# Row logits of a graph attention layer: turned on VectorE in 32x32 blocks instead of on TensorE

## The chip, the cores and the metric

The kernel runs on one core of a Trainium2 chip. The metric is the device time of one execution in microseconds (us). The engines are named as in the profile: PE is TensorE (PEld its weight loads), DVE is VectorE, ACT is ScalarE, POOL is GpSimd, SP is SyncE, which issues all the transfers that matter here.

## The reference

Two layers run over 64 graphs of 256 nodes with 512 features each. The first is a graph attention layer with 8 heads of 64 units, the second a transformer-like attention with the adjacency added to its probabilities. Each ends in a residual and a layer norm. The first layer is what the change touches:

```python
feats = jnp.einsum('bnf,hfu->bhnu', X, W)
e_self = jnp.einsum('bhnu,hu->bhn', feats, a_self)
e_neigh = jnp.einsum('bhnu,hu->bhn', feats, a_neigh)
dense = e_self[..., :, None] + e_neigh[..., None, :]
dense = jax.nn.leaky_relu(dense, negative_slope=0.2)
dense = dense + NEG_BIG * (1.0 - A[:, None, :, :])
att = jax.nn.softmax(dense, axis=-1)
out = jnp.einsum('bhij,bhju->bhiu', att, feats) + b[None, :, None, :]
...
x = _layernorm(x + _L0_gnn_ref(x, adj, ...), axis=-1)
x = _layernorm(x + _L1_gnn_ref(x, nodemask, adj, adj, ...), axis=-1)
```

Since the logit is a sum of one term per row and one per column, the exponential of the leaky sum is a product of a row factor and a column factor, and the larger of two such products. The kernel needs, for each head, the row factor exp(-0.8 (e_self + largest e_neigh)), limited to between 1e-30 and 1, on all 128 partitions, along the free dimension.

## The kernel before

Nodes lie on partitions in T = 2 tiles of 128 (P), features in C = 4 chunks. `proj0(b)` projects graph b for layer 0. Its result V0 holds, for each node and head, 64 features and two more columns: e_self and e_neigh. So the logits come out with nodes on partitions (columns), and the row factor must be turned so that nodes lie along the free dimension, and then be copied to all partitions.

From graph 2 on (62 graphs) this is done by these steps of `proj0`:

- `rows` (L551): eight matmuls against the identity write the logits of both kinds, turned, into a PSUM tile pr. Rows 0, 6, 12, ... hold e_self of the eight heads, rows 64 on hold e_neigh. VectorE takes the maximum (L560) and multiplies it by -0.8 (L561).
- `broadcast(0)` (L567): ScalarE takes the exponential, straight from PSUM, into the tile grow. The maximum rides along in its last column.
- `broadcast(1)` (L571 to L576): VectorE clamps grow. One transfer takes the eight rows to a DRAM buffer gs, a second one spreads gs over 128 partitions into gb (1 MB).
- `columns` (L645 on): nd is e_neigh less the maximum, and ScalarE makes the column factors ccol from it.
- `weights` of `attend0` (L741): VectorE makes the attention weights pT from gb, ccol and the adjacency; L764 multiplies them with v.

`shared` (L519 to L535) prepares the matrix ct of the second layer from the turned adjacency: part 0 is a sum and the tile even, part 1 two multiplications and another sum. `far` supplies exponentials of the adjacency for it.

The order of the work is written out by hand. `do(stage, b, step)` emits one step and `in_order` ties every instruction to the one before it on its engine, so each engine runs its instructions in the order of the source. `attention0_beside_projections1(b)` and `attention1_beside_projections0(b)` alternate for b from 2 to 63; one pair is one period of the kernel. A period works on four graphs at once: layer 0 of one, the projections of the next, and the layer-1 softmax and output of two earlier ones. In `second_beside_first` stands the order around the first of the 62 uses. The steps around the change, by their lines: `values` of `attend1` (L1054, av) and its copy oT (L1062); `scores` (L925, pz) and its exponentials (L944, p); `half_blocks` (L304 to L310, the sums oC of oT); `product` of `attend1` (L87, po, with the copies o at L340); `both` (L956) and its row sums pd (L964); `turned` xT (L130). Layer norms take three small POOL instructions each (L394 to L398), with the mean at L377.

Matrix products of the projections run as seven half-size products (`seven`), of which four in a row add into one PSUM bank; ScalarE copies the partial sum out between two of them, and the next product waits for that copy.

All DMA issues are on SP, in the order of the source: for one period the hidden rows hs out and back in blocks (hb), gs, gb, the next adjacency adj and mask, the reciprocals rs and their spread rb, the output, y, x and xb.

PSUM tiles of the kind that pr has come from a ring of four (tag mm).

Of the kernel before, what the change touches and what calls it, by code (L numbers as in the profile page):

```python
# [8 lines left out]
FT = mybir.dt.float32  # L9
BF = mybir.dt.bfloat16  # L10
U8 = mybir.dt.uint8
AF = mybir.ActivationFunctionType
ALU = mybir.AluOpType
AX = mybir.AxisListType
# [3 lines left out]
def kernel(  # L18
# [29 lines left out]
    nc = tc.nc  # L48
    P = 128
    NB, N, F = x.shape  # L50
    H, _, U = w0.shape
    T = N // P
# [3 lines left out]
    UX = U + 2  # L56
    W = 6
    R = W * (H - 1) + 1
    NEG = 1e10
    HIDE = 2.0**100  # L60
    TINY = 1e-30
# [4 lines left out]
    consts = ctx.enter_context(tc.tile_pool(name="consts", bufs=1))  # L66
# [10 lines left out]
    def ps_tile(shape, name):  # L77

        return psum.tile(shape, FT, tag="mm", name=name, bufs=4)

    matmul = nc.tensor.matmul
# [35 lines left out]
    B = 32  # L117
    Q = P // B
# [83 lines left out]


    maskz = io.tile([NB, N], FT, tag="y", name="maskz", bufs=1)
    hide = consts.tile([P, T, NB], FT, name="hide")
    m33 = consts.tile([P, T, NB], FT, name="m33")
    MASK = {}
# [280 lines left out]
    def proj0(b):  # L488
# [25 lines left out]

        def shared(part=None):
            mrow = FAR[1]
            if part != 1:
                CT[b] = work.tile([P, T, N], FT, tag="ct", name=f"ct_{b}", bufs=3)
                nc.vector.tensor_add(CT[b], pa, FAR[0])  # L519
                FAR[2] = work.tile([P, N], FT, tag="far", name=f"even_{b}", bufs=1)  # L520
                nc.vector.tensor_scalar(
                    FAR[2], mrow, -LA / N, LA / N, op0=ALU.mult, op1=ALU.add
                )
            if part == 0:
                return
            for j in range(T):
                nc.vector.scalar_tensor_tensor(
                    CT[b][:, j, :],
                    CT[b][:, j, :],
                    m33[:, j, b : b + 1],  # L530
                    mrow,
                    op0=ALU.mult,
                    op1=ALU.mult,
                )
            nc.vector.tensor_add(  # L535
                CT[b], CT[b], FAR[2].unsqueeze(1).to_broadcast([P, T, N])
            )
# [6 lines left out]
                nc.scalar.copy(xT[:, :, t * P : (t + 1) * P], pt)  # L544

        def rows():
            pr = ps_tile([P, N], f"pr_{b}")
            for t in range(T):
                for s in range(2):
                    cols = V0[b][:, t].rearrange("p h u -> p (h u)")  # L550
                    matmul(  # L551
                        pr[s * U : s * U + R, t * P : (t + 1) * P],
                        cols[:, U + s : U + s + UX * (H - 1) + 1 : UX // W],
                        ident,
                        start=True,
                        stop=True,
                    )
            grow = small.tile([R, N + 1], FT, tag="grow", name=f"grow_{b}", bufs=1)
            nb = small.tile([R, 1], FT, tag="nb", name=f"nb_{b}", bufs=2)
            nc.vector.tensor_reduce(grow[:, N : N + 1], pr[U : U + R], AX.X, ALU.max)  # L560
            nc.vector.tensor_scalar_mul(nb, grow[:, N : N + 1], -0.8)  # L561
            ROW.update(logits=pr, rows=grow, shift=nb)

        def broadcast(part):
            grow = ROW["rows"]
            if part == 0:
                nc.scalar.activation(  # L567
                    grow[:, :N], ROW["logits"][:R], AF.Exp, bias=ROW["shift"], scale=-0.8
                )
                return  # L570
            nc.vector.tensor_scalar(  # L571
                grow[:, :N], grow[:, :N], 1.0, TINY, op0=ALU.min, op1=ALU.max
            )
            gs = dram.tile([H, N + 1], FT, tag="gs", name=f"gs_{b}")
            nc.sync.dma_start(gs, grow[0:R:W])
            nc.sync.dma_start(  # L576
                gb.rearrange("p h n -> p (h n)"),
                gs.rearrange("h n -> (h n)").partition_broadcast(P),
            )
# [11 lines left out]
                )  # L591

        def cleared():
            ROW["rows"] = small.tile([P, N + 1], FT, tag="grow", name=f"grow_{b}", bufs=1)
            nc.gpsimd.memset(ROW["rows"], 0.0)

        def maxima(part=None):

# [98 lines left out]
        def scaled(h):  # L697
# [15 lines left out]
            xT_rows=from_rows,  # L713
            aT=lambda: transpose_blocks(pa, ADJB[b]),
            rows=rows,
            broadcast=broadcast,
            columns=columns,
            far=far,
# [497 lines left out]
    def do(stage, b, step, *args):  # L1216

        if 0 <= b < NB:
            if (stage, b) not in S:
                S[stage, b] = stages[stage](b)  # L1220
            S[stage, b][step](*args)
            in_order()

    def start():
# [120 lines left out]
        for h in range(HG, H):  # L1345
            do("attend0", 1, "weights", h)
        do("proj0", 0, "shared", 1)
        do("proj0", 1, "far", 1)
        load_adj(2)
        do("proj1", 0, "qk", "p4")  # L1350
# [4 lines left out]
    def second_beside_first():  # L1355


        b = 1
        for g in range(2):
            for t in range(T):  # L1360
                do("attend0", b, "product", g, t)
        do("attend0", b, "rec0", 0)
        do("attend0", b, "rec0", 1)
        load_rowmask()
        nc.sync.dma_start(bo_bc, b_out.partition_broadcast(P))
        WO["12"] = load_wo()
        do("turned", 2, "xT")
        do("turned", 2, "xC")
        do("attend0", b, "norm0", 0, 0)
        do("proj1", 0, "values", "p1")  # L1370
        do("attend0", b, "norm0", 0, 1)
        for t in range(T):
            do("attend0", b, "norm0", 1, t)
        do("proj1", 0, "values", "p2")
        do("proj1", 0, "v_add", 11)
        do("attend0", b, "end")
        right_factors(wf_sb, wf12, (0, 1, 2))
        do("proj1", 0, "values", "p6")
        do("proj1", 0, "values", "p5")
        do("proj1", 0, "values", "p7")  # L1380
        do("proj1", 0, "v_add", 22)
        right_factors(wf_sb, wf12, (3,))
        load(3)
        do("proj0", 2, "product", "p1")
        do("proj1", 0, "values", "p4")
        do("attend0", b, "squares", slice(0, 1), False)
        do("proj0", 2, "product", "p6")
        do("attend0", b, "squares", slice(1, 2), slice(0, 2))
        do("proj1", 0, "values", "p3")
        do("proj0", b, "shared")  # L1390
        do("proj0", 2, "aT")
        do("proj1", 0, "v_add", 12)
        do("proj0", 2, "product", "p5")
        do("proj0", 2, "product", "p7")
        do("attend0", b, "norm")
        do("proj1", b, "blocks")
        do("proj0", 2, "add", 22)
        do("proj0", 2, "product", "p2")
        do("proj0", 2, "product", "p4")
        do("proj0", 2, "far")  # L1400
        do("proj0", 2, "product", "p3")
        do("proj0", 2, "add", 11)
        do("proj0", 2, "add", 12)
        do("proj1", b, "from_rows", 0)
        do("proj1", b, "from_rows", 1)
        do("proj0", 2, "shared", 0)
        do("proj0", 2, "rows")
        do("proj0", 2, "broadcast", 0)
        do("softmax1", 0, "scores", 0)
        do("proj0", 2, "broadcast", 1)  # L1410
        load_adj(3)
        do("softmax1", 0, "scores", 1)
        do("proj0", 2, "shared", 1)
        do("proj1", b, "hC")
        do("softmax1", 0, "both", 0)
        do("softmax1", 0, "scores", 2)
        do("softmax1", 0, "both", 1)
        do("softmax1", 0, "scores", 3)
        do("softmax1", 0, "both", 2)
        do("turned", 3, "xT")  # L1420
        do("softmax1", 0, "both", 3)
        do("proj1", b, "qk", "p1")
        do("proj1", b, "qk", "p2")
        do("proj0", 2, "bias")
        do("softmax1", 0, "sums")
        do("softmax1", 0, "invert")
        do("proj0", 2, "columns")
        do("softmax1", 0, "inverted")
# [85 lines left out]
    def attention1_beside_projections0(b):  # L1514


        do("attend1", b - 2, "values", 0)
        do("attend1", b - 2, "values", 1)
        do("proj0", b + 1, "shared", 0)
        do("proj0", b + 1, "rows")  # L1520
        do("attend1", b - 2, "values", 2)
        do("attend1", b - 2, "values", 3)
        do("proj0", b + 1, "broadcast", 0)
        do("softmax1", b - 1, "scores", 0)
        do("proj0", b + 1, "shared", 1)
        if b + 2 < NB:
            do("turned", b + 2, "xT")
        do("proj0", b + 1, "broadcast", 1)
        if b + 2 < NB:
            load_adj(b + 2)  # L1530
        do("softmax1", b - 1, "scores", 1)
        do("attend1", b - 2, "half_blocks", 0)
        do("softmax1", b - 1, "both", 0)
        do("attend1", b - 2, "half_blocks", 1)
        do("softmax1", b - 1, "scores", 2)
# [153 lines left out]
```

## Time and profile before

| | us |
|---|---|
| median of 3 runs | 2828.33 |
| lowest, highest | 2826.14, 2829.4 |
| the profiled execution, whole | 2827.07 |
| its span, first to last instruction | 2825.3 |
| period of the steady part | 43.12 |

| engine | busy us | share of the span |
|---|---|---|
| PE | 2802.8 | 99% |
| PEld | 2238.0 | 79% |
| DVE | 2564.2 | 91% |
| ACT | 1811.0 | 64% |
| POOL | 257.3 | 9% |

In a row of the groups, the columns are: line, engine and operation, output and inputs by name, shapes, count; then the busy time and the mean nanoseconds of one; then the idle time of the engine before them, with what ended it. In the timeline a line gives start, length, engine, line and names; the bracket at the end is the idle time before it and its releaser. Instructions of one engine overlap by some 0.08 us at their ends, so the distance from one start to the next is the cost to the engine, and it is a little less than the length.

### The profile page before, as it was taken

How to read it: one execution, taken by the hardware profiler on the slowest of the kernel's cores; microseconds unless marked ns; L12 is line 12 of the kernel's file. 1: busy time of each engine (PE TensorE's matmuls, PEld its weight loads, DVE VectorE, ACT ScalarE, POOL GpSimd, SP SyncE). 2: the span in 40 equal slices, each digit the busy share in tenths (PEclk: the TensorE clock that was granted, in tenths of full speed). 3: DMA queues.
4: the chain of work that ended last, by engine and by line, in shares of the span. 5: the costliest groups of instructions: out<-in, count | busy, mean ns of one | idle time of the engine just before them, and what ended most of it. 6: DMA issues, size and time to landing. Idle time of an engine off the chain costs nothing.

```text
span 2825.3 us, 93442 instructions
## 1 busy us (share of the span) xinstructions
PE 2802.8 (99%) x39080; PEld 2238.0 (79%) x39080; DVE 2564.2 (91%) x5140; ACT 1811.0 (64%) x5051; POOL 257.3 (9%) x534
## 2 busy tenths in 40 slices
PE   9999999999999999999999999999999999999998
PEld 7878878788787788788787877887878878778785
DVE  7999999999999999999999999999999999999984
ACT  4666666666666666666666666666666666666663
POOL 1000100010010001000100100010001001000101
PEclk9999999999999999999999999999999999999999
DMA  7444545445545445445455454454554544544531
GB/s 141 121 106 136 134 125 141 122 133 143 123 126 139 121 135 136 125 139 122 133 143 123 125 139 122 133 137 125 139 122 133 144 121 128 137 123 132 133 107 67
DMA packets 772433, 362.56 MB, mean 128 GB/s; under 512 B 688319, under 2 KB 690351, under 8 KB 756014
## 3 DMA queue, kind: packets, MB, share of 16 engines
q1 hardware_dynamic: 769902, 356.07, 48.1%
q8 instruction: 310, 5.08, 0.8%
q14 instruction: 109, 0.89, 0.1%
q10 hardware_dynamic: 2112, 0.52, 0.1%
HBM read 288.11 MB, written 68.13 MB: 126 GB/s over the span
## 4 chain that ended last, share of the span: by engine, by line
PE 96%; DVE 1%; DMA 1%; SPq 1%; ACT 1%; issue 0%; POOL 0%; DVEq 0%; POOLq 0%
PE pq_p L87 27%; PE po_p L87 14%; PE pf_p L87 14%; PE pv_p L87 13%; PE av L764 8%; PE pz L925 8%; PE av L1054 7%; PE pd L964 2%; PE pr L551 1%; PE po L87 0%; SPq L265 0%; DMA rb<-rs 0%; DMA wo_sb<-in_L_gnn_W_out_dram 0%; SPq L244 0%; SPq L123 0%
## 5 line engine op out<-in xcount | busy, mean ns | idle before, releaser
L87 PE MATMUL pq_p<-hC,wqk_sb 128*64 128x128 f32 x8192 | 470.7, 273 | 3.1 <-DVE wqk_sb L283 1.6
L87 PEld LDWEIGHTS pq_p<-hC,wqk_sb 128*64 128x64 f32 x8192 | 449.1, 137 | 5.0 <-issue 3.1
L741 DVE SCALAR_TENSOR_TENSOR pT<-gb,ccol,at 128x256 f32<-128x256 f32 x992 | 403.0, 477 | 17.2 <-ACT ccol L652 17.2
L87 PE MATMUL pq_p<-hT,wqk_sb 128*64 128x128 f32 x6144 | 358.2, 273 | 0.3 <-DVE qk L343 0.3
L87 PEld LDWEIGHTS pq_p<-hT,wqk_sb 128*64 128x64 f32 x6144 | 342.5, 137 | 10.3 <-issue 0.8
L944 ACT ACTIVATE p<-pz,hide 128x512 f32<-128x512 f32 x638 | 333.7, 629 | 8.0 <-PE pz L925 1.0
L1035 DVE TENSOR_TENSOR p<-p,rb 128x1024 f32<-128x1024 f32 x252 | 299.2, 1208 | 4.8 <-DMA rb<-rs 4.8
L1044 DVE TENSOR_TENSOR p<-p,ct 128x1024 f32<-128x1024 f32 x252 | 299.0, 1207 | 0.2
L785 ACT ACTIVATE x<-av,rec 128x64 f32<-128x64 f32 x1024 | 224.6, 336 | 64.3 <-DVE rec L777 64.3
L764 PE MATMUL av<-v,pT 128*64 128x65 f32 x8192 | 253.5, 222 | 1.3 <-issue 0.7
L87 PE MATMUL pf_p<-wf_sb,xC 128*64 128x264 f32 x1984 | 254.5, 386 | 0.0
L700 ACT ACTIVATE v<-v 128x64 f32<-128x64 f32 x1024 | 251.3, 337 | 2.6 <-DVE v L691 2.6
L764 PEld LDWEIGHTS av<-v,pT 128*64 128x64 f32 x8192 | 249.7, 138 | 3.4 <-issue 2.4
L87 PE MATMUL pv_p<-wv_sb,hC 128*64 128x256 f32 x2048 | 245.3, 380 | 3.7 <-ACT v L340 3.7
L340 ACT COPY qk<-pq_p 128x512 f32<-128x512 f32 x256 | 149.0, 582 | 152.7 <-PE pq_p L87 150.0
L1054 PE MATMUL av<-p,v 128*64 128x256 f32 x2016 | 240.6, 379 | 2.1 <-DVE p L1044 2.1
L925 PE MATMUL pz<-qk 64*128 64x256 f32 x2048 | 238.7, 383 | 0.0
L340 ACT COPY v<-pv_p 128x256 f32<-128x256 f32 x256 | 95.6, 373 | 222.0 <-PE pv_p L87 222.0
L394 POOL TENSOR_SCALAR rstd_l<-rstd_l 128x2 f32<-128x2 f32 (+1 forms) x130 | 96.8, 744 | 1534.1 <-ACT junk L383 1533.9
L87 PE MATMUL po_p<-wo_sb,oC 128*64 128x256 f32 x1984 | 235.2, 379 | 0.0
L925 PEld LDWEIGHTS pz<-qk 64*128 64x128 f32 x2048 | 192.3, 186 | 45.0 <-issue 24.6
L956 DVE SCALAR_TENSOR_TENSOR both<-p 128x512 f32<-128x512 f32 x256 | 172.4, 674 | 44.6 <-ACT p L944 44.2
(172 smaller groups left out, 4460.9 us busy)
## 6 DMA issues: line engine op xcount, KB each, us to landing
rb<-rs SPq DMA_DIRECT2D x63, 1024.0 KB
gb<-gs SPq DMA_DIRECT2D x62, 1028.0 KB
hs<-x SPq DMA_DIRECT2D x64, 512.0 KB
xb<-in_x_dram SPq DMA_DIRECT2D x252, 128.0 KB
x<-in_x_dram SPq DMA_DIRECT2D x63, 512.0 KB
y<-hs SPq DMA_DIRECT2D x63, 512.0 KB
out_dram<-y SPq DMA_DIRECT2D x63, 512.0 KB
hb<-hs SPq DMA_DIRECT2D x248, 128.0 KB
```

The source lines that it names most:

```text
L87: matmul(dst[cols], lhsT[:, cols], rhs, **flags)
L340: nc.scalar.copy(out[COPIES[p]], dst)
L700: nc.scalar.activation(v[:, :U], v[:, :U], AF.Copy, scale=v[:, U : U + 1])
L741: nc.vector.scalar_tensor_tensor(pT[h][:, j, :], GB[b][h], CCOL[b][:, j, h : h + 1], AT[b][:, j, :], op0=ALU.max, op1=ALU.mult,)
L764: matmul(av[r * half : (r + 1) * half, k, :], pT[h][:, j, i : i + half], V0[b][:, j, h, :UA], start=(j == 0), stop=(j == T - 1),)
L785: nc.scalar.activation(X1[b][:, t, h * U : (h + 1) * U], av[:, k, :U], AF.Copy, scale=REC0[g][:, t, k : k + 1],)
L925: matmul(pz[r][:, j, :], QK[b][rows, g, 1, j * P : (j + 1) * P], QK[b][rows, g, 0, :], start=True, stop=True,)
L944: nc.scalar.activation(to, of, AF.Exp, bias=hide[:, j, b : b + 1], scale=U**-0.5,)
L956: nc.vector.scalar_tensor_tensor(both[g], p[:, :, 0, :], TINY, p[:, :, 1, :], op0=ALU.add, op1=ALU.add)
L1035: nc.vector.tensor_mul(p, p, REC[b][:, k : k + 2, g // 2, :] .unsqueeze(2) .to_broadcast([P, 2, T, N]),)
L1044: nc.vector.tensor_add(p, p, CT[b].unsqueeze(1).to_broadcast([P, 2, T, N]))
L1054: matmul(av[0][r * U : (r + 1) * U, g % 2, :], V1[b][:, j, 2 * g + r, :], PROBS[b][g][:, r, j, :], start=(j == 0), stop=(j == T - 1),)
```

## The change

The eight matmuls and their PSUM tile are gone. VectorE copies the logits of all nodes from V0 into a tile of its own (col_t: two kinds, two node tiles, 32 columns of which 8 are heads), and turns it in 32x32 blocks into row_t. There, heads lie on the first 8 partitions of each of four quarters of 32 partitions, and each quarter holds a fourth of the nodes of each tile. VectorE reduces each quarter's e_neigh to a maximum; POOL copies the four quarters side by side on the first 32 partitions; VectorE reduces these to the maximum (`top`), in a new step `shift`; POOL multiplies it by -0.8 four times, once for each quarter, and a transfer takes the maximum to gs. ScalarE's exponential and the clamp then work on 128 partitions of 64 elements instead of 43 of 256. The rows go to gs in four transfers, one for each quarter.

The order moves too. `shared` has a third part, the last sum alone. `rows` comes ahead of `shared` part 0; then follow `scores` 0, `shared` 1, `shift`, `shared` 2, and only then the exponential, after those of `scores` 0. The clamp and the transfers to gs and gb, with the loads of adj and mask behind them, come after xT, the exponentials of `scores` 1 and the first three sums of `half_blocks`. In the first period hC is split in two, around the clamp. The tile grow becomes a constant, shared with the two graphs at the start.

```diff
+    grow_sb = consts.tile([P, N + 1], FT, name="grow_sb")
+    col_t = grow_sb[:, : N // 2].rearrange("p (s t h) -> p s t h", s=2, t=T)
+    row_t = grow_sb[:, N // 2 : N].rearrange("p (s t r) -> p s t r", s=2, t=T)
...
         def rows():
-            pr = ps_tile([P, N], f"pr_{b}")
-            for t in range(T):
-                for s in range(2):
-                    cols = V0[b][:, t].rearrange("p h u -> p (h u)")
-                    matmul(
-                        pr[s * U : s * U + R, t * P : (t + 1) * P],
-                        cols[:, U + s : U + s + UX * (H - 1) + 1 : UX // W],
-                        ident,
-                        start=True,
-                        stop=True,
-                    )
-            grow = small.tile([R, N + 1], FT, tag="grow", name=f"grow_{b}", bufs=1)
-            nb = small.tile([R, 1], FT, tag="nb", name=f"nb_{b}", bufs=2)
-            nc.vector.tensor_reduce(grow[:, N : N + 1], pr[U : U + R], AX.X, ALU.max)
-            nc.vector.tensor_scalar_mul(nb, grow[:, N : N + 1], -0.8)
+            if b == 2:
+                nc.gpsimd.memset(col_t, 0.0)
+            nc.vector.tensor_copy(
+                col_t[:, :, :, :H],
+                V0[b][:, :, :, U:].rearrange("p t h s -> p s t h"),
+            )
+            nc.vector.transpose(
+                row_t.rearrange("p s t r -> p (s t r)"),
+                col_t.rearrange("p s t h -> p (s t h)"),
+            )
+            quarter = small.tile([P, 1], FT, tag="quarter", name=f"quarter_{b}", bufs=2)
+            nc.vector.tensor_reduce(
+                quarter, row_t[:, 1].rearrange("p t r -> p (t r)"), AX.X, ALU.max
+            )
+            quarters = small.tile([B, Q], FT, tag="quarters", name=f"quarters_{b}", bufs=2)
+            for q in range(Q):
+                nc.gpsimd.tensor_copy(
+                    quarters[:, q : q + 1], quarter[q * B : (q + 1) * B]
+                )
+
+        def shift():
+            top = small.tile([B, 1], FT, tag="top", name=f"top_{b}", bufs=2)
+            nc.vector.tensor_reduce(top, ROW["quarters"], AX.X, ALU.max)
+            nb = small.tile([P, 1], FT, tag="nb", name=f"nb_{b}", bufs=2)
+            for q in range(Q):
+                nc.gpsimd.tensor_scalar_mul(nb[q * B : (q + 1) * B], top, -0.8)
+            gs = dram.tile([H, N + 1], FT, tag="gs", name=f"gs_{b}")
+            nc.sync.dma_start(gs[:, N : N + 1], top[:H])
 
         def broadcast(part):
             if part == 0:
-                nc.scalar.activation(
-                    grow[:, :N], ROW["logits"][:R], AF.Exp, bias=ROW["shift"], scale=-0.8
-                )
+                nc.scalar.activation(grow, grow, AF.Exp, bias=ROW["shift"], scale=-0.8)
                 return
-            nc.sync.dma_start(gs, grow[0:R:W])
+            nc.vector.tensor_scalar(grow, grow, 1.0, TINY, op0=ALU.min, op1=ALU.max)
+            for q in range(Q):
+                nc.sync.dma_start(
+                    gs[:, :N].rearrange("h (t q r) -> q h t r", q=Q, r=B)[q],
+                    grow[q * B : q * B + H],
+                )
...
     def attention1_beside_projections0(b):
+        do("proj0", b + 1, "rows")
         do("proj0", b + 1, "shared", 0)
-        do("proj0", b + 1, "rows")
         do("attend1", b - 2, "values", 2)
         do("attend1", b - 2, "values", 3)
-        do("proj0", b + 1, "broadcast", 0)
         do("softmax1", b - 1, "scores", 0)
         do("proj0", b + 1, "shared", 1)
+        do("proj0", b + 1, "shift")
+        do("proj0", b + 1, "shared", 2)
+        do("proj0", b + 1, "broadcast", 0)
         if b + 2 < NB:
             do("turned", b + 2, "xT")
+        do("softmax1", b - 1, "scores", 1)
+        do("attend1", b - 2, "half_blocks", 0)
         do("proj0", b + 1, "broadcast", 1)
         if b + 2 < NB:
             load_adj(b + 2)
-        do("softmax1", b - 1, "scores", 1)
-        do("attend1", b - 2, "half_blocks", 0)
```

More of the change, by code (lines that the diff above doesn't have):

```diff
@@ L516, in shared @@
             mrow = FAR[1]
-            if part != 1:
+            if part in (None, 0):
                 CT[b] = work.tile([P, T, N], FT, tag="ct", name=f"ct_{b}", bufs=3)
@@ L525, in shared @@
                 return
-            for j in range(T):
+            for j in range(T) if part != 2 else ():
                 nc.vector.scalar_tensor_tensor(
@@ L534, in shared @@
                 )
+            if part == 1:
+                return
             nc.vector.tensor_add(
@@ L558, in rows @@
-            grow = small.tile([R, N + 1], FT, tag="grow", name=f"grow_{b}", bufs=1)
-            nb = small.tile([R, 1], FT, tag="nb", name=f"nb_{b}", bufs=2)
-            nc.vector.tensor_reduce(grow[:, N : N + 1], pr[U : U + R], AX.X, ALU.max)
-            nc.vector.tensor_scalar_mul(nb, grow[:, N : N + 1], -0.8)
-            ROW.update(logits=pr, rows=grow, shift=nb)
+            if b == 2:
[4 more added lines that the diff above has]
+            )
@@ new lines, in rows @@
+            ROW.update(quarters=quarters)
+        def shift():
[6 more added lines that the diff above has]
+            nc.sync.dma_start(gs[:, N : N + 1], top[:H])
+            ROW.update(shift=nb, dram=gs)
@@ L564, in broadcast @@
         def broadcast(part):
-            grow = ROW["rows"]
+            grow = row_t[:, 0]
             if part == 0:
-                nc.scalar.activation(
-                    grow[:, :N], ROW["logits"][:R], AF.Exp, bias=ROW["shift"], scale=-0.8
-                )
-                return
-            nc.vector.tensor_scalar(
-                grow[:, :N], grow[:, :N], 1.0, TINY, op0=ALU.min, op1=ALU.max
-            )
-            gs = dram.tile([H, N + 1], FT, tag="gs", name=f"gs_{b}")
-            nc.sync.dma_start(gs, grow[0:R:W])
+                nc.scalar.activation(grow, grow, AF.Exp, bias=ROW["shift"], scale=-0.8)
+                return
@@ L576, in broadcast @@
+            nc.vector.tensor_scalar(grow, grow, 1.0, TINY, op0=ALU.min, op1=ALU.max)
+            gs = ROW["dram"]
+            for q in range(Q):
+                nc.sync.dma_start(
+                    gs[:, :N].rearrange("h (t q r) -> q h t r", q=Q, r=B)[q],
+                    grow[q * B : q * B + H],
+                )
             nc.sync.dma_start(
@@ L593, in cleared @@
         def cleared():
-            ROW["rows"] = small.tile([P, N + 1], FT, tag="grow", name=f"grow_{b}", bufs=1)
-            nc.gpsimd.memset(ROW["rows"], 0.0)
+            ROW["rows"] = grow_sb
+            nc.gpsimd.memset(grow_sb, 0.0)
         def maxima(part=None):
@@ L715, in proj0 @@
             rows=rows,
+            shift=shift,
             broadcast=broadcast,
@@ L1347, in start @@
         do("proj0", 0, "shared", 1)
+        do("proj0", 0, "shared", 2)
         do("proj0", 1, "far", 1)
@@ L1407, in second_beside_first @@
         do("proj0", 2, "rows")
+        do("softmax1", 0, "scores", 0)
+        do("proj0", 2, "shared", 1)
+        do("proj0", 2, "shift")
+        do("proj0", 2, "shared", 2)
         do("proj0", 2, "broadcast", 0)
-        do("softmax1", 0, "scores", 0)
+        do("softmax1", 0, "scores", 1)
+        do("proj1", b, "hC", (0, 2))
         do("proj0", 2, "broadcast", 1)
         load_adj(3)
-        do("softmax1", 0, "scores", 1)
-        do("proj0", 2, "shared", 1)
-        do("proj1", b, "hC")
+        do("proj1", b, "hC", (1, 3))
         do("softmax1", 0, "both", 0)
```

## The prediction

> **What bounds the kernel now.** I read the busy shares first, then the chain that ended last, then the groups of instructions, then the timeline of one period.
>
> ```profile
> span 2825.3 us, 93442 instructions
> ...
> PE 2802.8 (99%) x39080; PEld 2238.0 (79%) x39080; DVE 2564.2 (91%) x5140; ACT 1811.0 (64%) x5051; POOL 257.3 (9%) x534
> ...
> PE 96%; DVE 1%; DMA 1%; SPq 1%; ACT 1%; issue 0%; POOL 0%; DVEq 0%; POOLq 0%
> ```
>
> TensorE is busy 99% of the span and carries 96% of the chain; the chain's line shares give 1% to the row logits at L551 (the figure "PE pr L551 1%"). So work taken from TensorE shortens the kernel, as long as nothing else becomes late. The groups, kept apart by shape:
>
> ```profile
> L551 PE MATMUL pr<-ident,v 128*43 128x128 f32 x496 | 38.4, 273 | 0.0
> L560 DVE TENSOR_REDUCE grow<-pr 43x1 f32<-43x256 f32 x62 | 26.4, 426 | 2.0
> L567 ACT ACTIVATE grow<-pr,nb 43x256 f32<-43x256 f32 x62 | 29.1, 469 | 0.6 <-DVE nb L561 0.6
> L571 DVE TENSOR_SCALAR grow<-grow 43x256 f32<-43x256 f32 x62 | 15.1, 244 | 1.2 <-ACT grow L567 1.2
> ```
>
> There are 62 graphs with these steps. The chain, in order of time, repeats every 43.12 us, so one period stands for all. Its part around the change, in the timeline (start, length, engine):
>
> ```profile
> 1281.20 0.42 DVE L343 TENSOR_TENSOR v<-pf_p,v 128x264 f32<-128x264 f32 x1
> ...
> 1282.00 0.61 PE L551 MATMUL pr<-ident,v 128*43 128x128 f32 x8
> ...
> 1282.44 1.90 PE L1054 MATMUL av<-p,v 128*64 128x256 f32 x16
> ...
> 1284.38 0.59 ACT L1062 COPY oT<-av 128x512 f32<-128x512 f32 x1 [1.58 <-PE av L1054]
> ...
> 1284.86 0.47 ACT L567 ACTIVATE grow<-pr,nb 43x256 f32<-43x256 f32 x1
> 1285.44 3.88 ACT L944 ACTIVATE p<-pz,hide 128x512 f32<-128x512 f32 x8
> ...
> 1289.17 0.42 ACT L340 COPY o<-po_p 128x256 f32<-128x256 f32 x1
> ```
> ```profile
> 1289.64 2.36 PEld L87 LDWEIGHTS po_p<-wo_sb,oC 128*64 128x64 f32 x24 [0.23 <-ACT o L340]
> ```
>
> The second thing to see is that ScalarE is full from 1284.38 to 1289.59, and TensorE's next weight load starts 0.05 us after it, having waited 0.23. TensorE loses nothing yet, but there is no slack: **this stretch of ScalarE is a second bound**, and it holds the exponential that the change moves.
>
> **What the Trainium skill says.** (1) "SBUF — State Buffer", Who interferes with whom: a VectorE instruction with two SBUF inputs and a GpSimd instruction that reads SBUF exclude each other; the later one waits for the whole of the other. The trace agrees:
>
> ```profile
> 1276.26 1.18 DVE L1044 TENSOR_TENSOR p<-p,ct 128x1024 f32<-128x1024 f32 x1
> 1276.43 1.07 POOL L394 TENSOR_SCALAR rstd_l<-rstd_l 128x2 f32<-128x2 f32 x1 [4.88 <-ACT junk L383]
> ```
> L394 is 1.07 us here, though its shortest is 0.19; it ends 0.06 after VectorE's instruction. (2) "VectorE: DVE Perf Modes", The three transpose paths: VectorE turns separate 32x32 blocks only. That is why the maximum ends up in four quarters of 32 partitions. No line of before shows how a maximum crosses partitions on GpSimd. (3) "DMA: Bandwidth & Descriptors", Anatomy of one DMA, puts about 2 us of fixed cost on a transfer, nearly all completion (stated for DMAs issued by GpSimd). For SyncE's the trace has 1.74 us from the issue of rs to that of rb, which waits for it (1297.32 and 1299.05), and 2.44 from gs to gb.
>
> **The change, part by part** (times in this period's frame).
>
> *TensorE loses eight matmuls.* 1282.44 - 1282.00 = 0.44 us from the first of them to the next av. 62 x 0.44 = **27 us**. The busy time says 0.62 each (38 us), but that counts the pipeline's overlap with av; 27 is the price, 38 the upper end. The PSUM buffer of pr falls away too; the ring of four turns on by one, each buffer's previous user is then an earlier or equal one, so I cost that at nothing.
>
> *VectorE's rows step.* Removed: the reduce 0.43 and the scale 0.15. Added: a copy of 32 elements, about 0.17 (168 ns for the 16-element nd); a transpose of 128, worked from 1.24 us for 1024 and 0.71 for 512 elements as 0.17 + 1.04 x 0.128 = 0.30; a reduce of 64, 0.17 + 0.06 = 0.24; the reduce of four, 0.18 at most. The clamp shrinks from 0.24 to 0.14, with 64 elements instead of 256. Sum +0.89 - 0.68 = +0.2 us per period, or 13 in all, on an engine 9% idle (3.9 us a period). It waits 0.68 us for ScalarE at L956 just after, which absorbs it, so nothing. If that cover is gone, the row sums pd (1292.39) are next late; both for its last matmuls is ready at 1291.78.
>
> *When the shift is ready.* The v addition ends at 1281.62. Copy 1281.65, transpose 1281.85, reduce 1282.19 to 1282.43. POOL's four copies then meet the ct addition (0.69, two SBUF inputs, to 1283.1). I take 0.20 us each: L377, a scalar multiply like the new ones, has a median of 0.22, and back to back they start 0.17 apart. So the quarters are there between 1283.8 and 1284.3 (if the other ct instructions hold them too); VectorE's own order reaches the last reduce at 1284.24. No wait, or 0.1. It ends at 1284.45; behind it on VectorE stand the second ct addition, xT and the oC that po needs. The second ct addition (L535 of before, two inputs again) holds the first of POOL's four multiplies to 1285.0, the other three take 0.2 each under the xT transpose (one input): **shift ready 1285.6**, bounds 1285.3 and 1286.2.
>
> *ScalarE.* Everything from the second oT copy on comes 0.44 earlier with TensorE: oT 1283.94, two exponentials (0.58 apart) 1284.48 and 1285.06. The rows' exponential may start at 1285.63, as the shift arrives; behind its wait stand the other exponentials and the o copy that TensorE waits for. With 64 elements it takes 0.25 of the engine (L700, 64 wide: sixteen in 3.92) instead of 0.58 to the next. The o copy then starts at 1288.45, i.e. 0.72 earlier, where TensorE asks for 0.44. So the shift may be 0.3 late before TensorE loses anything.
>
> *SyncE and the broadcast.* The clamp moves past xT and three oC: 1287.04 to 1287.19, was 1286.13. The maximum's transfer goes out behind hb's last issue (to 1286.39), under that. Then four issues for one. Nearest rows: rs 0.56, gs 0.69, adj 0.66; bounds 0.37 (out) and 0.69; I take 0.62. The last starts at 1289.1; +1.74 until it has landed, +0.2 for six waits: gb issued at **1291.05** instead of 1288.93. The packets of gb end 5.4 us after issue (median) and the one wait for it shows 0.6 more: there at 1297.0. nd needs it at 1297.52 - 0.44 = 1297.08. It fits by 0.1 in the middle and not in some periods; but behind nd ScalarE's two short ones, squares and POOL's shift end 0.61 before the y pass at 1301.10, so up to 0.6 late costs nothing. Queued behind gb on SyncE: adj and mask end at 1297.3 instead of 1295.2, and rs is due at 1296.9: 0.4 late. rb is used 4.5 us after its packets end (median), so nothing. adj is needed 20 us on.
>
> *The first of the 62* has its own order (hC split in two around the clamp): once, under 1 us either way.
>
> **Sum.** The profiled execution took 2827.1 us (span 2825.3, 1.8 around it), 1.3 below the median of 2828.3. 2827.1 - 27 + 0 = 2800; against the median **2801 us**.
>
> **Rivals.** *Partial gain*: the shift comes 0.5 to 0.6 late, or gb 0.8 to 0.9 late; 0.2 to 0.3 of the 0.44 is lost. For it: eight POOL instructions on other partitions than they write have no row here. Against: the 0.3 spare. 62 x 0.25 = 15 back: 2817. *No change*: the loss happens to equal 0.44: 2828. *Slower*: the xT transpose, 1.24 us, also holds GpSimd off SBUF. Then the second multiply ends at 1286.15, the next two behind oC subtractions (two inputs): shift at 1286.85, 1.2 late, 0.9 lost against 0.44 won: 62 x 0.45 = +28, **2856**. It decides from 0.75 us late (0.3 + 0.44), that is if POOL's multiplies cost over 0.4 each. For it: L394's wait above. Against: the page counts two inputs or a mode that this transpose's rate, 1.04 ns an element, does not show; and no POOL row lies under a turn in a steady period.
>
> **Chances.** Full gain 0.55 (2796 to 2808), partial 0.17 (2808 to 2822), no change 0.07, slower 0.21. A measurement of this kernel tells about 0.2% (5.7 us) from none, so faster means below 2822.6: 0.72, same 0.07, slower 0.21. The range: 2795 (the removed group's overlap paying a little more) to 2834, which leaves out the slower rival.
>
> **What would show it.** Right: a period of 42.7 us in the chain; no PE L551; ScalarE's rows exponential idle before it under 0.3 us; gb to nd without waits over 0.6; PE idle before po and before the next av unchanged. Wrong: "ACT grow <- POOL nb" of over 0.3 us a time with PE waiting for ACT o; or DVE nd waiting for gb by a microsecond in most periods, and PE av for ACT v; or POOL instructions of over 0.4 us.

## The result, and the profile after

The changed kernel takes 2815.03 us (median of 5), against 2829.17 for the kernel before beside it: ratio 0.9953, interval 0.9939 to 0.9968. That is 14 us less, where the prediction had 27. Its profiled execution is the longest of the five, 2818.2 us.

The head of the page of the changed kernel, and the shares of its chain:

```profile
span 2816.4 us, 93444 instructions
...
PE 2791.7 (99%) x38584; PEld 2201.8 (78%) x38584; DVE 2561.5 (91%) x5264; ACT 1801.3 (64%) x5051; POOL 417.8 (15%) x1031
...
PE 94%; DVE 2%; ACT 1%; DMA 1%; issue 1%; SPq 0%; POOL 0%; DVEq 0%; POOLq 0%; ACTq 0%
```

PE has 496 instructions fewer: the eight matmuls of 62 graphs are gone. But its share of the chain has fallen from 96% to 94%, so something else now ends waits. The period in the chain is 42.92 us, 0.21 shorter than before, where the price of the matmuls was 0.44. So **0.23 us a period came back** (62 x 0.23 = 14 us). The waits say where; the columns are the total, the number of times and the longest:

```profile
ACT p L965 <- PE pz L946: 31.3, 64, 1.2
...
PEld po_p L87 <- ACT o L343: 29.3, 62, 0.8
```

Before, these two were 1.0 and 14.5. The second one is TensorE's weight load at po, which waits for ScalarE's copy o: now 0.47 us a time instead of 0.23. The first is new: ScalarE waits 0.48 us a time for pz. One period in the timeline of the changed kernel:

```profile
1279.01 0.42 DVE L346 TENSOR_TENSOR v<-pf_p,v 128x264 f32<-128x264 f32 x1
...
1281.64 3.72 PE L946 MATMUL pz<-qk 64*128 64x256 f32 x32
1281.76 0.58 ACT L1083 COPY oT<-av 128x512 f32<-128x512 f32 x1 [1.14 <-PE av L1075]
...
1282.15 0.69 DVE L540 TENSOR_TENSOR ct<-ct,even 128x512 f32<-128x512 f32 x1
1282.26 1.46 POOL L579 TENSOR_SCALAR nb<-top 32x1 f32<-32x1 f32 x4 [0.50 <-DVE top L576]
1282.76 1.24 DVE L130 STREAM_TRANSPOSE xT<-xb 128x1024 f32<-128x1024 f32 x1
1282.83 1.26 ACT L965 ACTIVATE p<-pz,hide 128x512 f32<-128x512 f32 x2 [0.48 <-PE pz L946]
...
1283.98 0.35 ACT L587 ACTIVATE grow_sb<-grow_sb,nb 128x64 f32<-128x64 f32 x1
1284.22 2.72 ACT L965 ACTIVATE p<-pz,hide 128x512 f32<-128x512 f32 x6
...
1285.30 1.95 PE L87 MATMUL po_p<-wo_sb,oT 128*64 128x256 f32 x16
...
1286.78 0.42 ACT L343 COPY o<-po_p 128x256 f32<-128x256 f32 x1
...
1287.25 2.36 PEld L87 LDWEIGHTS po_p<-wo_sb,oC 128*64 128x64 f32 x24 [0.47 <-ACT o L343]
1287.26 2.81 PE L87 MATMUL po_p<-wo_sb,oC 128*64 128x256 f32 x24
...
1290.00 1.07 PE L985 MATMUL pd<-both,ones 128*32 128x256 f32 x16
```

Read ScalarE from top to bottom. The copy oT ends at 1282.34; then it stands idle for 0.48 us until pz is there. Then two exponentials, the rows' exponential (L587, no wait ahead of it: the shift was ready), six more, and the copy o, which po is waiting for. Now TensorE in the same stretch of the kernel before:

```profile
1284.26 3.72 PE L925 MATMUL pz<-qk 64*128 64x256 f32 x32
...
1287.92 1.95 PE L87 MATMUL po_p<-wo_sb,oT 128*64 128x256 f32 x16
...
1289.69 2.76 PE L87 MATMUL po_p<-wo_sb,oC 128*64 128x256 f32 x24
...
1292.39 1.07 PE L964 MATMUL pd<-both,ones 128*32 128x256 f32 x16
```

There pz's first matmul started at 1284.26 and the first exponential at 1285.44, 1.18 later; here it is 1281.64 and 1282.83, which is 1.18 again before rounding. So the wait for pz was there before as well. It did not show, because the rows' exponential stood in it: oT from 1284.38, grow from 1284.86, p from 1285.44. The kernel before even has the bare wait: its last two graphs in layer 1 have no rows' exponential beside them, and there p waits 0.48 us for pz, just as in the changed kernel. These two are the whole 1.0 us of its list:

```profile
2749.17 3.73 PE L925 MATMUL pz<-qk 64*128 64x256 f32 x32
2749.28 0.59 ACT L1062 COPY oT<-av 128x512 f32<-128x512 f32 x1 [0.39 <-PE av L1054]
...
2750.35 3.88 ACT L944 ACTIVATE p<-pz,hide 128x512 f32<-128x512 f32 x8 [0.48 <-PE pz L925]
```

**The change moved the rows' exponential out of a gap, in which it cost nothing, into a stretch without slack.** There its 0.24 us (1283.98 to 1284.22) go onto the copy o and so onto TensorE. From pz's first matmul to that of the row sums pd it was 8.13 us (1284.26 to 1292.39) and is now 8.36 (1281.64 to 1290.00): the whole 0.23 is lost in this stretch.

### The profile page after: what moved, and what is told of

The parts are those of the page before. It is cut to its first block, busy times and chain, and to the rows that moved or that the text cites. A ratio compares the mean times of both kernels' runs of the same rounds, so it can differ in the third digit from the quotient of the medians.

```text
span 2816.4 us, 93444 instructions
## 1 busy us (share of the span) xinstructions
PE 2791.7 (99%) x38584; PEld 2201.8 (78%) x38584; DVE 2561.5 (91%) x5264; ACT 1801.3 (64%) x5051; POOL 417.8 (15%) x1031
## 4 chain that ended last, share of the span: by engine, by line
PE 94%; DVE 2%; ACT 1%; DMA 1%; issue 1%; SPq 0%; POOL 0%; DVEq 0%; POOLq 0%; ACTq 0%
PE pq_p L87 27%; PE po_p L87 14%; PE pv_p L87 13%; PE pf_p L87 13%; PE av L785 8%; PE pz L946 8%; PE av L1075 7%; PE pd L985 2%; PE po L87 0%; ACT p L965 0%; SPq L268 0%; DVE p L1065 0%; DVE p L1056 0%; DMA x<-in_x_dram 0%; DMA gb<-gs 0%
## 5 line engine op out<-in xcount | busy, mean ns | idle before, releaser
L965 ACT ACTIVATE p<-pz,hide 128x512 f32<-128x512 f32 x638 | 339.5, 625 | 31.3 <-PE pz L946 31.3
L1075 PE MATMUL av<-p,v 128*64 128x256 f32 x2016 | 230.3, 380 | 2.5 <-DVE p L1065 2.5
L87 PEld LDWEIGHTS pv_p<-wv_sb,hC 128*64 128x64 f32 x2048 | 153.5, 137 | 73.6 <-ACT v L343 4.8
```

The lines of the kernel that those rows point to most:

```text
L87: matmul(dst[cols], lhsT[:, cols], rhs, **flags)
L965: nc.scalar.activation(to, of, AF.Exp, bias=hide[:, j, b : b + 1], scale=U**-0.5,)
L1075: matmul(av[0][r * U : (r + 1) * U, g % 2, :], V1[b][:, j, 2 * g + r, :], PROBS[b][g][:, r, j, :], start=(j == 0), stop=(j == T - 1),)
```

## The experiments

The theory (S) is the sentence in bold. The rivals are the shift's path over VectorE and GpSimd (V) and SyncE with the later broadcast (Q).

**The exponential put back into the gap.** The bias becomes a constant, so that the exponential may run that early; the largest e_neigh is then missing from the row factor.

```diff
-                nc.scalar.activation(grow, grow, AF.Exp, bias=ROW["shift"], scale=-0.8)
+                nc.scalar.activation(grow, grow, AF.Exp, bias=mhalf[:, :1], scale=-0.8)
...
+        do("proj0", b + 1, "broadcast", 0)
         do("softmax1", b - 1, "scores", 0)
         do("proj0", b + 1, "shared", 1)
         do("proj0", b + 1, "shift")
         do("proj0", b + 1, "shared", 2)
-        do("proj0", b + 1, "broadcast", 0)
```

> The changed kernel, with the rows' exponential ahead of the exponentials of scores 0 again, where ScalarE waits for pz anyway. So that it can run there, its bias is a constant -0.5: the maximum is left out of the row factor, though all its instructions still run. Theory S (the exponential now stands inside the full stretch of ScalarE between pz and the copy o, and costs TensorE its own 0.24 us a period): those 0.24 disappear, po's first stretch is 1.78 us again, period 42.69, about 2801 us. Rival V (what is lost comes from the shift's path: VectorE's four steps, POOL's eight instructions, and their contention): these still run in the same places, so the time stays near 2815. Rival Q (SyncE's five issues and the later broadcast): the clamp is not moved, so 2815 too.

Measured: 2799.18 us, ratio to before 0.9901 (0.9887 to 0.9914); period 42.69. Its timeline, for ScalarE and the product po:

```profile
1316.13 0.58 ACT L1083 COPY oT<-av 128x512 f32<-128x512 f32 x1 [1.14 <-PE av L1075]
1316.61 0.35 ACT L587 ACTIVATE grow_sb<-grow_sb,mhalf 128x64 f32<-128x64 f32 x1
1317.20 3.88 ACT L965 ACTIVATE p<-pz,hide 128x512 f32<-128x512 f32 x8 [0.23 <-PE pz L946]
1319.67 1.95 PE L87 MATMUL po_p<-wo_sb,oT 128*64 128x256 f32 x16
1320.91 0.42 ACT L343 COPY o<-po_p 128x256 f32<-128x256 f32 x1
```

The exponential sits between oT and p, and ScalarE still has 0.23 us to wait for pz. TensorE is not late: the whole 0.44 is won. All the instructions of V and Q still ran. What this run takes away of V is the exponential's wait for the shift, but that wait is only 2.9 us in the whole changed kernel. So neither explains the loss of 14 us. The full price of the matmuls, 27 us, was right.

**The new order alone, with the old rows.**

```diff
-        do("proj0", b + 1, "broadcast", 0)
         do("softmax1", b - 1, "scores", 0)
         do("proj0", b + 1, "shared", 1)
+        do("proj0", b + 1, "broadcast", 0)
         if b + 2 < NB:
             do("turned", b + 2, "xT")
-        do("proj0", b + 1, "broadcast", 1)
-        if b + 2 < NB:
-            load_adj(b + 2)
         do("softmax1", b - 1, "scores", 1)
         do("attend1", b - 2, "half_blocks", 0)
+        do("proj0", b + 1, "broadcast", 1)
+        if b + 2 < NB:
+            load_adj(b + 2)
```

> The kernel before with its eight matmuls, its maximum and its one transfer, but in the changed kernel's order: the rows' exponential after those of scores 0, the clamp and the transfers after the first three sums of half_blocks. Theory S: the exponential of 256 columns takes about 0.37 us of ScalarE from one start to the next; placed behind pz's wait it delays the copy o by that, less the 0.05 spare: 62 x 0.32 = 20 us slower than before, about 2849 us (2843 to 2853). Rivals V and Q: nothing of the new path is there, so 2829 as before, at most 3 us more from the later broadcast.

Measured: 2846.09 us against 2826.72, ratio 1.0068 (1.0055 to 1.0082): 19 us slower, as S said. The period is 43.43, 0.31 longer. Its waits and its ScalarE:

```profile
PEld po_p L87 <- ACT o L340: 33.3, 62, 0.5
...
ACT p L944 <- PE pz L925: 31.1, 63, 1.3
```
```profile
1293.80 3.72 PE L925 MATMUL pz<-qk 64*128 64x256 f32 x32
...
1294.98 1.26 ACT L944 ACTIVATE p<-pz,hide 128x512 f32<-128x512 f32 x2 [0.48 <-PE pz L925]
1296.13 0.46 ACT L567 ACTIVATE grow<-pr,nb 43x256 f32<-43x256 f32 x1
1296.49 2.69 ACT L944 ACTIVATE p<-pz,hide 128x512 f32<-128x512 f32 x6
```

The 0.48 us wait comes out as soon as the old exponential leaves its place, with nothing of the new path in the kernel. The exponential takes 0.36 us of ScalarE (1296.13 to 1296.49). TensorE's weight load at po waits 0.54 us a time for the copy o instead of 0.23. That is the whole loss of a period, so the later broadcast adds nothing that shows.

**The copy o ahead of the last exponential of scores 2.** `exponentials` is split so that three of the four pieces come first.

```diff
-        do("softmax1", b - 1, "scores", 2)
+        do("softmax1", b - 1, "scores", 2, 0)
+        do("softmax1", b - 1, "scores", 2, 2)
         do("softmax1", b - 1, "both", 1)
         do("softmax1", b - 1, "scores", 3, 0)
         do("attend1", b - 2, "product", "p1")
+        do("softmax1", b - 1, "scores", 2, 3)
         do("softmax1", b - 1, "scores", 3, 1)
```

> The changed kernel, with ScalarE's first copy o moved ahead of the last of the four exponentials of scores 2; nothing else moves, and the result is complete. Theory S: the copy starts 0.36 us earlier, more than the 0.23 lost in a period; po's first stretch 1.78, po's second 2.69, period 42.69, about 2801 us. Rivals V and Q: the copy is not what is late, so 2815; or slower by up to 0.1 us a period (2821) since both of group 2 waits 0.4 longer for its last exponential.

Measured: 2800.49 us, ratio to before 0.9905 (0.9892 to 0.9919); period 42.69. **This version beats both kernels** and leaves nothing out. Its timeline around po:

```profile
1319.06 2.35 ACT L972 ACTIVATE p<-pz,hide 128x512 f32<-128x512 f32 x5
...
1320.14 1.95 PE L87 MATMUL po_p<-wo_sb,oT 128*64 128x256 f32 x16
...
1321.27 0.41 ACT L343 COPY o<-po_p 128x256 f32<-128x256 f32 x1
1321.54 1.67 ACT L972 ACTIVATE p<-pz,hide 128x256 f32<-128x256 f32 x3
...
1321.91 2.76 PE L87 MATMUL po_p<-wo_sb,oC 128*64 128x256 f32 x24
```

From po's start to its second stretch it is 1.77 us, as in the kernel before (1287.92 to 1289.69); in the changed kernel it is 1.96 (1285.30 to 1287.26). That 0.19 (the exponential's 0.24, less the 0.05 by which po's weight load ran ahead of its matmuls before) is most of the 0.23; the rest is in the second stretch, up to pd (2.70 us before, 2.74 in the changed kernel; why it is longer is not shown). With the copy early both are gone: the late copy is thus the loss.

**The same move in the kernel before**, as a control; the diff is the one above.

> The kernel before with the same move of the copy o ahead of the last exponential of scores 2. Theory S: TensorE loses nothing at this copy in the kernel before (its weight load waits 0.23 us, its matmuls do not), so no change, 2829 within 3 us. If instead the copy alone were worth 14 us anywhere, it would show here: 2815.

Measured: 2828.12 us against 2826.72, ratio 1.0007 (0.9998 to 1.0015): no change. The copy is worth something only where it is late.

**The matmuls of the row logits twice**, in the kernel before.

```diff
-                    matmul(
-                        pr[s * U : s * U + R, t * P : (t + 1) * P],
...
+                    for _ in range(2):
+                        matmul(
+                            pr[s * U : s * U + R, t * P : (t + 1) * P],
...
```

> The kernel before, with each of the eight matmuls of the row logits issued twice. This measures the first term of the sum by itself. If a group of eight costs the 0.44 us from its start to that of the next matmul, the time rises by 62 x 0.43 to 0.44 = 27 us, to about 2855. If it costs its busy time (0.62, 38 us): 2866. If part of it is hidden by a wait elsewhere, less than 27.

Measured: 2858.53 us against 2827.7, ratio 1.011 (1.0093 to 1.0127): 31 us more. In its timeline:

```profile
1297.16 1.12 PE L552 MATMUL pr<-ident,v 128*43 128x128 f32 x16
...
1298.04 1.98 PE L1055 MATMUL av<-p,v 128*64 128x256 f32 x16
...
1299.94 3.72 PE L926 MATMUL pz<-qk 64*128 64x256 f32 x32
```

The sixteen take 0.88 us (1297.16 to 1298.04), 0.44 for each eight. The period is 43.64, 0.52 longer: some 0.08 more is lost in av just after them (1.90 us from av to pz, against 1.82 before), for a reason that stays open. Removing the first eight did not give such a part back (0.44 in the first and third experiment). So the price by the distance of starts holds for the removal. Doubling them costs a little more, but less than the busy time would have it (38 us).

**GpSimd's multiplies twice**, in the changed kernel.

```diff
-            for q in range(Q):
-                nc.gpsimd.tensor_scalar_mul(nb[q * B : (q + 1) * B], top, -0.8)
+            for q in range(2 * Q):
+                nc.gpsimd.tensor_scalar_mul(nb[q % Q * B : (q % Q + 1) * B], top, -0.8)
```

> The changed kernel, with each of GpSimd's four multiplies issued twice (eight, 0.265 us apart in the trace of the changed kernel). There the last multiply ends 0.26 us ahead of the rows' exponential. Four more end 1.06 later, so the exponential and all of ScalarE behind it start about 0.8 us later; TensorE is already late there, so nothing is left to hide it: 62 x 0.8 = 50 us, about 2865 (2855 to 2872). If the shift's path had a wide margin, or ScalarE's stretch had slack, the time would stay near 2815.

Measured: 2883.93 us, ratio to before 1.0198 (1.0183 to 1.0213): 69 us more than the changed kernel. The direction is right, the size was too small.

```profile
1314.08 2.79 POOL L579 TENSOR_SCALAR nb<-top 32x1 f32<-32x1 f32 x8 [0.50 <-DVE top L576]
...
1316.90 0.35 ACT L587 ACTIVATE grow_sb<-grow_sb,nb 128x64 f32<-128x64 f32 x1 [0.99 <-POOL nb L579]
...
1320.18 2.81 PE L87 MATMUL po_p<-wo_sb,oC 128*64 128x256 f32 x24 [1.12 <-ACT o L343]
```

Eight take 2.79 us instead of 1.46 for four, 1.33 more rather than 1.06. ScalarE waits 0.99 us for the shift and TensorE 1.12 for the copy o. The period is 44.02, 1.11 longer than the changed kernel's, and 62 x 1.11 = 69. So the shift had about 0.2 us to spare (1.33 less 1.11), and past that the whole of GpSimd's added time came out on TensorE in this run.

## Why the prediction was wrong

The direction, the bound and the place of the danger were right; the size was half. Step by step:

- **TensorE loses eight matmuls, 0.44 each, 27 us.** Right: the exponential in the gap and the earlier copy both give a period of 42.69, 0.44 less than 43.12 before rounding, and 2799 to 2800 us.
- **The step that failed is in the part on ScalarE: "two exponentials (0.58 apart) 1284.48 and 1285.06", and "it takes 0.25 of the engine ... instead of 0.58 to the next".** I took the whole 0.58 from the start of the old rows' exponential to that of the next as its cost, and so as time that its move would free. But 0.22 of it was the wait for pz: behind pz's wait the old exponential takes 0.36 from start to start (second experiment). And the other 0.36 ran inside that same wait, so its move freed nothing. My first exponential started 0.66 us after pz's first matmul (1283.82, which is 1284.26 less 0.44); it starts 1.18 after it, in the kernel before as in the one after. From there on my sum ran 0.5 us early. Counted from pz's first matmul, the copy o came at 4.91 us before; I had 4.63, and so 0.3 us to spare; it comes at 5.14 (1281.64 to 1286.78). That is 0.23 later in place of 0.28 earlier: the rows' exponential adds its 0.24 behind pz's wait, and nothing falls away ahead of it. I had written that this stretch has no slack, and then booked the exponential's move as a saving in it.
- Why I did not see it: the kernel before shows only 1.0 us of waits of p for pz, and I read ScalarE as full from 1284.38 on. A wait that is filled by other work is not in the view of waits. Two signs of it were there. ScalarE is idle for 0.11 us between the end of the rows' exponential and p (1285.33 to 1285.44; where nothing waits, the next one starts some 0.1 before the end, as in the second experiment, so this agrees with the 0.22). And the 1.0 us are two waits of 0.48, both at the places where no rows' exponential comes before p.
- **VectorE's rows step.** Right to within 0.05 us: copy 0.19, transpose 0.31, reduce 0.22, last reduce 0.14. The clamp is 0.19 rather than 0.14. The lengths of all VectorE's instructions add up to 13 us more over the span, as I had; its busy time, which counts overlaps once, is 3 us less.
- **The shift.** Within its bounds. It was predicted ready 4.0 us after the end of the v addition (1281.62 to 1285.6, bounds 3.7 to 4.6); GpSimd's four multiplies end at 1282.26 + 1.46 = 1283.72, which is 4.3 us after the addition's end (1279.01 + 0.42 = 1279.43). The rows' exponential did not wait for it (2.9 us in all the 62, in 2 places).
- **The slower rival** (xT holds GpSimd off SBUF). It did not happen: under xT, from 1282.76, three multiplies take 0.2 us each (the median of all 248 is 0.206). The ct addition, with two SBUF inputs, did hold the first, as the Trainium skill has it ("SBUF — State Buffer", Who interferes with whom): all four take 1.46 us instead of some 1.0 (by 0.2 for one and starts 0.27 apart). But a late shift does cost what this rival said in kind: with the doubled multiplies the kernel is 56 us slower than the kernel before (2883.93 less 2827.7).
- **SyncE and the broadcast.** Priced too high: four issues of rows take 0.29 us each (median), not 0.62, below the lower bound that I gave. From gb's issue to nd it is 7.7 us in the median instead of 8.6, and nd waits for gb twice in the whole run, 1.5 us in all.

The partial gain that I named (2817) has the right time by luck, and not for its reason: neither the shift nor the broadcast was late.

## What to carry to other kernels

Before moving an instruction on an engine that runs in order, find out whether it stands in a wait that its neighbour has anyway: measure the neighbour's start from the producer's start, not from the end of what precedes it, and look for places in the same trace where the neighbour runs without the instruction (here the last two graphs). An engine busy for 64% of the span can bind for four microseconds in each period, and there a quarter of a microsecond is paid in full. When a gain comes out at half, look for the copy or the load that the bounding engine now waits for, and move that one ahead; here it took a few lines of the order.

## What the runs showed of the hardware

- The first exponential of scores 0 starts 1.18 us after the first matmul of pz (1284.26 to 1285.44, 1281.64 to 1282.83, 1293.80 to 1294.98). The traces of all eight kernels have it so, in each of 61 periods. Which of pz's matmuls it waits for, the trace does not tell, and it wasn't tried.
- A transfer of 8 partitions by 64 elements is issued in 0.29 us (median of 248), where that of 8 by 257 took 0.69.
- GpSimd multiplies and copies of 32x1 elements have medians of 0.206 and 0.177 us. The multiplies that lie wholly under the 32x32-block transpose xT on VectorE (180 of the 248) take 0.20 to 0.21 us.
